# The last image's end in a four-layer hybrid network: buffers in the freed scan memory, interleaved spectral halves, and evictions split between ScalarE and VectorE

## The chip, the cores and the metric

The kernel runs on one core of one Trainium2 chip. The metric is the device time of one execution in microseconds, from launch to end; lower is better. Three runs of the kernel before took 6479.0, 6490.46 and 6488.11 us, so its median is 6488.11 us.

The engines are named as the profile names them: PE is TensorE with its matmuls, PEld its weight loads, DVE is VectorE, ACT is ScalarE, POOL is GpSimd, SP is SyncE, whose queue issues all the loads and stores here.

## What is computed

Four images of 96 channels and 64 x 64 pixels go through four layers. In short:

```python
# layer 0: group norm, input projection and 3x3 convolution, four selective scans
h = h * exp(delta * A) + (delta * u) * B;  y = sum(h * C)      # 4 directions, 192 channels, 16 states, 4096 steps
x = x + Wout @ layer_norm(y0 + y1 + y2 + y3)
# layer 1: inverted bottleneck
x = x + bn(w2 @ relu(bn(depthwise3x3(relu(bn(w1 @ x))))))
# layer 2: spectral mixing over the 4096 tokens, then a feed-forward with numbers rounded to 8 bits
X = fft(relu(bn(layer_norm(t) @ w1)))
t = t + bn(ifft(relu(X.real*rd - X.imag*id + rb) + 1j*relu(X.imag*rd + X.real*id + ib)).real @ w2)
t = t + ffn(layer_norm(t))       # relu(q(q(x) @ q(W1)) + q(b1)), then the same with W2
# layer 3: attention without softmax, so (q k^T) v = q (k^T v), then the second feed-forward
t = t + attention(layer_norm(t)); t = t + ffn(layer_norm(t))
```

## The kernel before

**Tiling.** An image is cut into 8 chunks of 512 pixels (8 rows of 64). Channels lie on partitions, pixels on the free axis; the layer-0 scan puts 32 channel pairs times 4 states on the 128 partitions.

**The long part.** `scans` walks over all scan units of all four images. POOL makes the products `db` (L1215) and half of `hc` (L1254), ACT the decays (L1225), DVE the scans (L1234) and the other half of `hc` (L1239), PE sums the states (L1275). This part stands under a hand-made order: everything else of the images (`front`, `turn`, `conv_block`, `spectral`, `layers_2_and_3`) is written as generators that yield their cost per engine, and `advance` slips their steps in beside the scan. Each of these groups of generators is a `Stage` with a width, the number of streams that run at a time.

**The end.** When the scan of the last image is over, three things are left: the rest of `conv_block` of that image, and all of its layers 2 and 3. `force` issues these steps in turn. `alone` is set by then: it gives the small products all eight PSUM banks (`turns`), and it picks other code in a few places. In this part the order on each engine is no longer by hand; the framework's scheduler places the instructions. `spare` says from where the fp32 temporaries `tmp` come: before, from the pool `beside` (tag `tmp`, ten buffers, which also hold all 8-bit and 16-bit temporaries) and from the scan's own tags `rep_d`, `rep_BC` and `hc`, of which each gives half a buffer. That is why scan names stand in rows of the last stages.

**conv_block.** A block `c` is two chunks (16 rows). `scan_outputs` makes the layer-0 result of a chunk (loads of `ypart` L679, sums L696, norm L715 to L737) and stores it to `d_x1`. `expansions` loads the 18 rows that a block needs as `xin` (L773, trace name `wd<-x`), and makes 18 groups of hidden channels by L782 into a ring of eight. `rows` does the depthwise products L805, whose results ACT evicts by L811, then the projection L821 and L822, and L825 adds the input. There is one place for `xin`, so a block is loaded only when the one before is finished. `norms` then runs `layer_norm` (L858 centres, L861 squares, L864 averages, L154 and L155 make the reciprocal root by logarithm and exponential, L872 multiplies into `xp`).

**spectral.** A 4096-point transform is done as 64 x 64: five phases, each a run of `in_turn` (PE fills a bank, an engine evicts it, two in flight). L955 multiplies by `wa1`, DVE evicts to `d` (L959). L980 with table `r1` transforms, ACT evicts to `z` (L991). L999 multiplies by the 16 tables `etab`, ACT evicts with Relu to `f` (L1003). L980 with `r2`, ACT to `v` (L1011). L1021 with the 8 tables `gtab`, ACT to `y` (L1025). The tables are loaded by L973, 256 KB each, two ahead, into five buffers. The 192 channels go in two halves, one after the other. `big` gives two buffers of 24 KB per partition in turn, so the `y` of the first half is stored to `d_half` in HBM and loaded again by layer_2.

**layer_2 and layer_3.** layer_2 is one stream per chunk: L1043 and L1044 add both halves through `wa2`, `residual` (L928) adds the input, `feed_forward` runs (norm with L870 as its last step; L884 and L905 are the products; L887 and L908 move their sums to 16 bits; L892 and L911 add the biases; L898 on DVE or L901 on ACT rounds to 8 bits; L914 adds the residual), then a layer norm, the keys and values by L1055 and L1058, and their sum over all tokens in `vk` (L1064, L1070). `product` multiplies the small matrices once. layer_3 is again one stream per chunk: L1097, `residual`, `feed_forward`, store. Both have width 3.

Of the kernel before, what the change touches and what calls it, by code (L numbers as in the profile page):

```python
# [28 lines left out]
L = H * W  # L29
# [15 lines left out]
POOL_C = (1, 3, 6, 8, 10)  # L45
TMP, IN = 10, 5
# [48 lines left out]
def hybrid_kernel(ctx: ExitStack, tc: tile.TileContext, a: dict):  # L95
# [71 lines left out]
    sp = pool("scan", bufs=2)  # L167
    bp = pool("beside", bufs=2)

# [8 lines left out]

    def big(name):
        return bp.tile([128, 6144], F32, name=name, tag="big", bufs=2)  # L180
# [6 lines left out]
    def tmp(name, shape=(128, CH), dtype=F32):  # L187

        if alone and dtype == F32:
            tag = turns(spare)  # L190
            if tag in SCAN:
                return pair(tag)[:, 0, : shape[1]]
        return bp.tile(list(shape), dtype, name=name, tag="tmp", bufs=TMP)

    def arrival(name):

        return bp.tile([128, CH], F32, name=name, tag="in", bufs=IN)
# [543 lines left out]
    def conv_block(b):  # L741
# [9 lines left out]
        def memory():  # L751
            held["w"], held["h"] = big("wd"), big("h1")
            load(held["w"][:, : 6 * NG * 32].rearrange("p (g m) -> p g m", m=32), diags)
            ring = held["h"][:, : 8 * 8 * (W + 2)].rearrange("p (s r w) -> p s r w", s=8, r=8)
            held["wd"] = held["w"][:, : 6 * NG * 32].rearrange("p (g o x m) -> p g o x m", g=NG, o=2, x=3)
            held["ring"] = ring
            at = [(held["h"], 8 * 8 * (W + 2) + n * CH) for n in range(3)]
            at += [(held["w"], 6 * NG * 32 + 18 * (W + 2) + n * CH) for n in range(2)]
            held["spare"] = [t[:, lo : lo + CH] for t, lo in at]
            yield dv(0.3)  # L760
            for edge in (0, W + 1):
                nc.vector.memset(ring[:, :, :, edge : edge + 1], 0.0)

        def expansions():

            yield from memory()
            for c in reversed(range(NCH // 2)):

                while max(2 * c - 1, 0) not in done or held.get("xin") is not None:
                    yield wait(1)  # L770
                at = 6 * NG * 32
                xin = held["w"][:, at : at + 18 * (W + 2)].rearrange("p (r w) -> p r w", r=18)
                load(xin, d_x1[im][:, 16 * c : 16 * c + 18, :])  # L773
                held["xin"] = xin
# [15 lines left out]
        def rows(c):  # L790
            h2 = []
            for q, groups in enumerate(quads):
# [3 lines left out]
                xin, here = held["xin"], [h for h, _ in ready[first : first + len(groups)]]  # L796
# [34 lines left out]
            held["xin"] = None  # L831
# [6 lines left out]
        def blocks():  # L838
            for c in reversed(range(NCH // 2)):
                while held.get("xin") is None:  # L840
                    yield wait(1)
                yield from rows(c)
# [32 lines left out]
    def feed_forward(x, weights):  # L875
# [5 lines left out]
        for m in range(3):  # L881
# [14 lines left out]
            if alone and m == 1:  # L896
                yield dv(0.75)
                nc.vector.tensor_copy(hq[:, m, :], acc, saturate=False)  # L898
            else:
                yield ac(0.65)  # L900
                nc.scalar.activation(hq[:, m, :], acc, AF.Copy, saturate=False)  # L901
# [8 lines left out]
        yield ac(0.65)  # L910
        act(acc[:C], acc[:C], AF.Identity, bias=bq[:C, 3:4])  # L911
        if alone:
            yield dv(0.9)
            nc.vector.tensor_add(x[:C], x[:C], acc[:C])  # L914
            return
        yield pe(1.4, 1)
# [22 lines left out]

    def spectral(b, hh):  # L940
# [8 lines left out]

        d = big("d").rearrange("p (h n) -> p h n", h=C)  # L950
# [7 lines left out]
        def diagonal(p, g):  # L958
            nc.vector.scalar_tensor_tensor(  # L959
# [4 lines left out]
            if g == 0:  # L964
                for at in (0, 64):
                    one = d[at : at + 1, :, 0]
                    nc.vector.tensor_add(one, one, rib[at : at + 1, hs])

        yield from in_turn(range(16), pe(0.7, 1), times, dv(0.8), diagonal)

        def table(name, g, n):
            t = arrival("tab").rearrange("p (a b) -> p a b", a=n)
            load(t, a[name][:, g * n : g * n + n, :])  # L973
            return t

        def transform(of, r):
# [8 lines left out]
        tables = ahead(2, lambda g: table("etab", g, 4), range(16))  # L985
        first = next(tables)

        z = big("z").rearrange("p (k h) -> p k h", k=64)
        yield from in_turn(
            range(C // 8), pe(0.7, 1), transform(d, "r1"), ac(1.1),  # L990
            lambda p, g: nc.scalar.copy(z[:, :, g * 8 : g * 8 + 8], p.rearrange("p (h k) -> p k h", h=8)))  # L991


        f = big("f").rearrange("p (h k) -> p h k", h=C)

        def twiddled(p, of):
            g, tab = of
            for e in range(4):
                mm(p[:, e * C : (e + 1) * C], lhsT=tab[:, e, :], rhs=z[:, g * 4 + e, :], start=True, stop=True)  # L999

        yield from in_turn(
            chain([first], tables), pe(0.7, 1), twiddled, ac(0.9),
            lambda p, of: act(f[:, :, of[0] * 4 : of[0] * 4 + 4].rearrange("p h k -> p k h"),  # L1003
                              p[:, : 4 * C].rearrange("p (k h) -> p k h", k=4), AF.Relu))
        tables = ahead(2, lambda g: table("gtab", g, 8), range(8))
        first = next(tables)

        v = big("v").rearrange("p (n h) -> p n h", n=64)
        yield from in_turn(
            range(C // 8), pe(0.7, 1), transform(f, "r2"), ac(1.1),  # L1010
            lambda p, g: nc.scalar.copy(v[:, :, g * 8 : g * 8 + 8].rearrange("p n h -> p h n"),  # L1011
                                        p.rearrange("p (h n) -> p h n", h=8)))

        yf = big("y")[:, :L]
        y = yf.rearrange("p (a b) -> p a b", a=64)
        load(yf[C:], a["zeros"][: 128 - C])

        def back(p, of):
            g, tab = of
            for e in range(8):  # L1020
                mm(p[:C, e * 64 : (e + 1) * 64], lhsT=v[:, g * 8 + e, :], rhs=tab[:, e, :], start=True, stop=True)  # L1021

        yield from in_turn(
            chain([first], tables), pe(1.2, 1), back, ac(1.1),
            lambda p, of: nc.scalar.copy(y[:C, :, of[0] * 8 : of[0] * 8 + 8].rearrange("p a b -> p b a"),  # L1025
                                         p[:C].rearrange("p (b a) -> p b a", b=8)))
        halves_of[b] = yf
        if hh == 0:
            later(d_half[im], yf[:C])
# [3 lines left out]
    def layers_2_and_3(b):  # L1033
# [3 lines left out]
        def layer_2(c):  # L1037

            x, first = load_x(d_x2[im], c), load_x(d_half[im], c)
# [4 lines left out]
            mm(p[:C], lhsT=wa2[:, 1, :], rhs=halves_of[b][:, chunk(c)], start=False, stop=bool(alone))  # L1044
# [5 lines left out]
            for half, t in enumerate(kv):  # L1050
# [6 lines left out]
                yield ac(0.6)  # L1057
                nc.scalar.copy(t[:, : 4 * C], p[:, : 4 * C])  # L1058
# [33 lines left out]
        def layer_3(c):  # L1092
# [8 lines left out]

        return [
            Stage("spectral", 1, spectral(b, 0)),
            Stage("spectral", 1, spectral(b, 1)),
            Stage("layer_2", 3, *(layer_2(c) for c in range(NCH))),
            Stage("product", 1, product()),
            Stage("layer_3", 3, *(layer_3(c) for c in range(NCH))) if b not in (1, 2) else
# [324 lines left out]
    spare += ["tmp", "rep_d", "tmp", "rep_BC", "tmp", "hc"]  # L1432
# [150 lines left out]
```

## Time and profile before

| what | us |
| --- | --- |
| the three runs | 6479.0, 6490.46, 6488.11 |
| the profiled execution | 6478.26 |
| its span, first to last instruction | 6476.4 |
| busy in the span: PE, DVE, ACT, POOL | 4756.9, 5432.5, 4244.3, 5175.7 |
| last scan sum evicted (L1286) | 6009.3 to 6009.8 |
| conv_block's rest ends | 6166.7 |
| both spectral halves end | 6305.4 |
| layer_2 and product end | 6415.8 |
| last sum of layer_3; end of the span | 6472.9; 6476.4 |

The page gives busy time per engine over the whole span, and the same in 40 slices. A row of the timeline has a start, a duration, the engine, the line, output and inputs, the count and, in brackets, how long the engine was idle before it and who ended that. Line numbers are those of the kernel before. Where a group's row has a mean, instructions that follow each other closely may start less than that apart, because their records overlap: the spacing of starts is then the better price.

### The profile page before, as it was taken

Reading aid. Unit: us, or ns where it says so; the run is one execution under the profiler, and the core shown is the slowest. Engines: PE = TensorE matmul, PEld = TensorE weight load, DVE = VectorE, ACT = ScalarE, POOL = GpSimd, SP = SyncE. Lnnn points to the kernel's source line nnn. Section 1 sums busy time; section 2 is a strip of 40 time slices with the busy share of each in tenths; the row PEclk is TensorE's granted clock in tenths of the full one; section 3 lists DMA queues with packets and bytes.
Section 4 is the critical chain, followed back from the end, with each engine's and each line's share of the span. In section 5 each row is a group of like instructions: output and inputs, shape, how many; then the busy total and the mean of one; then the engine's idle time right before and its main releaser. Section 6 shows DMA issues by size and latency. Waiting matters only on the chain. (4 is left out here: it accounts for less than half of the span.)

```text
span 6476.4 us, 84592 instructions
## 1 busy us (share of the span) xinstructions
PE 4756.9 (73%) x27804; PEld 1748.4 (27%) x27804; DVE 5432.5 (84%) x5947; ACT 4244.3 (66%) x8152; POOL 5175.7 (80%) x2743
## 2 busy tenths in 40 slices
PE   7623867757987776775688877677887776758997
PEld 2100212111224521221122254211224621112383
DVE  5979998998999889989899998978998888898123
ACT  5743777865665677887466667756665676756356
POOL 4857878789998889987899988978999888899000
PEclk9755978868998887886799988888998877979998
DMA  5644565676544544466764455466644554655131
GB/s 191 206 154 145 187 208 191 202 236 232 179 156 160 172 165 151 162 202 200 241 214 160 151 183 179 159 214 192 186 156 154 173 168 168 204 189 162 34 100 39
DMA packets 438827, 1121.43 MB, mean 173 GB/s; under 512 B 73002, under 2 KB 74768, under 8 KB 437140
## 3 DMA queue, kind: packets, MB, share of 16 engines
q1 hardware_dynamic: 438388, 1116.02, 52.1%
q8 instruction: 221, 3.62, 0.2%
q14 instruction: 218, 1.79, 0.1%
HBM read 881.28 MB, written 239.01 MB: 173 GB/s over the span
## 5 line engine op out<-in xcount | busy, mean ns | idle before, releaser
L1215 POOL TENSOR_TENSOR db<-rep_g,rep_BC 128x1024 f32<-128x1024 f32 x1536 | 3597.3, 2364 | 344.3 <-DVE ps_da L1234 232.3
L1225 ACT ACTIVATE ps_da<-rep_d,aneg 128x512 f32<-128x512 f32 x3072 | 2062.5, 691 | 437.3 <-DVE hc L1234 323.1
L1234 DVE TENSOR_TENSOR_SCAN ps_da<-ps_da,state,db 128x512 f32<-128x512 f32 x1568 | 1923.9, 1272 | 314.8 <-ACT state L1249 209.9
L1254 POOL TENSOR_TENSOR hc<-hc,rep_BC 128x1024 f32<-128x1024 f32 x640 | 1511.8, 2362 | 110.4 <-DVE hc L1234 55.7
L1275 PE MATMUL ps_y<-hc,cst 128*32 128x512 f32 x6144 | 1009.2, 735 | 626.4 <-POOL hc L1254 366.7
L1234 DVE TENSOR_TENSOR_SCAN hc<-ps_da,state,db 128x512 f32<-128x512 f32 x1120 | 1371.3, 1265 | 108.2 <-issue 41.6
L1239 DVE TENSOR_TENSOR hc<-ps_da,rep_BC 128x512 f32<-128x512 f32 x1792 | 1134.9, 674 | 0.1
L1249 ACT COPY state<-ps_da 128x1 f32<-128x1 f32 x1568 | 246.9, 157 | 502.9 <-DVE hc L1239 493.4
L1275 PEld LDWEIGHTS ps_y<-hc,cst 128*32 128x32 f32 x6144 | 144.4, 117 | 1262.2 <-POOL hc L1254 748.8
L1251 POOL COPY state<-hc 128x2 f32<-128x2 f32 x560 | 105.9, 189 | 369.7 <-DVE hc L1234 352.4
L805 PE MATMUL ps_mm<-h,wd 128*32 128x512 f32 x3192 | 367.0, 595 | 8.3 <-ACT r L154 8.3
L543 PE MATMUL ps_mm<-xp,taps 128*128 128x512 f32 x576 | 296.2, 657 | 54.4 <-ACT ua L545 22.7
L1234 DVE TENSOR_TENSOR_SCAN ps_da<-ps_da,db 128x512 f32<-128x512 f32 x224 | 261.3, 1211 | 49.6 <-ACT state L1249 29.8
L782 PE MATMUL ps_mm<-wd,w 128*32 128x512 f32 x2128 | 273.8, 628 | 38.6 <-DMA wd<-x 25.1
L1286 ACT COPY yt<-ps_y 128x512 f32<-128x512 f32 x256 | 149.1, 583 | 163.7 <-PE ps_y L1275 159.2
L594 PE MATMUL ps_mm<-xd,dtw 128*128 128x512 f32 x256 | 165.5, 737 | 102.3 <-ACT z L616 55.9
L786 ACT ACTIVATE h<-ps_mm 128x512 f32<-128x512 f32 x266 | 153.4, 597 | 60.5 <-PE ps_mm L782 58.6
L955 PE MATMUL ps_mm<-wa,xp 128*64 128x96 f32 x1728 | 136.6, 317 | 76.4 <-DVE d L959 64.6
L864 PE MATMUL ps_mm<-r,cst 128*128 128x512 f32 x208 | 145.9, 790 | 63.5 <-ACT r L861 17.5
L1234 DVE TENSOR_TENSOR_SCAN hc<-ps_da,db 128x512 f32<-128x512 f32 x160 | 186.1, 1203 | 4.9 <-ACT ps_da L1225 3.3
L609 DVE SCALAR_TENSOR_TENSOR ps_mm<-ps_mm,z 128x512 f32<-128x512 f32 x192 | 131.7, 686 | 58.3 <-ACT z L607 55.0
L543 PEld LDWEIGHTS ps_mm<-xp,taps 128*128 128x128 f32 x576 | 115.5, 208 | 230.9 <-issue 159.7
(405 smaller groups left out, 6798.8 us busy)
## 6 DMA issues: line engine op xcount, KB each, us to landing
rep_BC<-bc SPq DMA_DIRECT2D x512, 512.0 KB
rep_g<-du SPq DMA_DIRECT2D x384, 512.0 KB
rep_d<-delta SPq DMA_DIRECT2D x384, 512.0 KB
y<-yt SPq DMA_DIRECT2D x512, 128.0 KB
du<-g SPq DMA_DIRECT2D x128, 256.0 KB
delta<-z SPq DMA_DIRECT2D x128, 256.0 KB
tab<-in_etab SPq DMA_DIRECT2D x128, 256.0 KB
ypart<-y SPq DMA_DIRECT2D x72, 256.0 KB
```

The costliest lines, as they stand in the source:

```text
L543: mm(p, lhsT=taps[:, t, 0:128], rhs=window(t, c + e), start=t == 0, stop=t == 8)
L594: mm(p, lhsT=dtw[:, o + 2 * part, 0:128], rhs=xd, start=True, stop=True)
L782: mm(p[32 * n : 32 * n + 32], lhsT=w1[:, 32 * g : 32 * g + 32], rhs=xin[:, n : n + 15 : 2, 1 : W + 1], start=True, stop=True)
L786: act(h[:, :, 1 : W + 1], split(p), AF.Relu)
L805: mm(p[32 * n : 32 * n + 32], lhsT=held["wd"][:, groups[i], o, dx, :], rhs=here[i][:, :, dx : dx + W], start=dx == 0, stop=dx == 2)
L1215: nc.gpsimd.tensor_mul(x["db"], x["step"]["g"][x["i"]], both(x["step"]["BC"][x["j"]][:, 0]))
L1225: act(x["da"][e], x["step"]["d"][x["i"]][:, e], AF.Exp, scale=aneg[:, av : av + 1])
L1234: nc.vector.tensor_tensor_scan(x["h"][e][:, order], x["da"][e][:, order], x["db"][:, e, order], start, ALU.mult, ALU.add)
L1239: x["made"] = nc.vector.tensor_mul(x["hc"][:, e], x["h"][e], x["step"]["BC"][x["j"]][:, 1])
L1249: nc.scalar.copy(to[:, e : e + 1], x["h"][e][:, end : end + 1])
L1254: x["made"] = nc.gpsimd.tensor_mul(x["hc"], x["hc"], both(x["step"]["BC"][x["j"]][:, 1]))
L1275: done = mm(y[32 * q : 32 * q + 32], lhsT=const("stack"), rhs=x["hc"][:, e], start=first or (x["pass"] == 0 and x["j"] == 0), stop=last or ...
```

## The change

Only what runs behind the last scan is rewritten; the code before it has the same operations.

- The pool `scan` now lies above the pool `beside` and is closed after the last scan. In its place a pool `last` is opened, with 24 table buffers, 6 more fp32 temporaries, two buffers for `xin` and one more `big`.
- `conv_block` takes `xin` from this pool in the rest, so that two blocks may be in memory at once; `held["xin"]` becomes a dict by block.
- The three `big` buffers let both spectral halves go through the five phases together, phase by phase, first half then second half. Each table is loaded once, into its own buffer, and used by both. Both results stay in SBUF: the store to `d_half` and its loads go.
- Of the evictions to `z`, `f`, `v` and `y`, the odd ones move to DVE.
- In the feed-forward all casts to 8 bits go to DVE, as well as the last bias; the copies of keys and values go to DVE too.
- The last image's layer_2 and layer_3 have width 4.
- Temporaries of layers 2 and 3 come from the `tab` and `more` buffers.
- The scratch memory for DMAs issued by POOL is set to 1024 bytes.

In the instruction lists POOL is unchanged. In the rest of `conv_block` SP loads the first `xin`, then all 24 tables in a row, then makes the stores of `o` and of chunk 0 and loads the second `xin`.

```diff
+LAST = {"tab": 24, "more": 6}
...
-    sp = pool("scan", bufs=2)
     bp = pool("beside", bufs=2)
+    scan_room = ExitStack()
+    sp = scan_room.enter_context(tc.tile_pool(name="scan", bufs=2))
+    last_room = []
...
+    thirds = ["last", "beside", "beside"]
     def big(name):
+        if last_room and turns(thirds) == "last":
+            return last_room[0].tile([128, 6144], F32, name=name, tag="big", bufs=1)
         return bp.tile([128, 6144], F32, name=name, tag="big", bufs=2)
...
-        if alone and dtype == F32:
+        if last_room and dtype == F32:
             tag = turns(spare)
-            if tag in SCAN:
-                return pair(tag)[:, 0, : shape[1]]
+            if tag in LAST:
+                return last_room[0].tile([128, CH], F32, name=name, tag=tag, bufs=LAST[tag])[:, : shape[1]]
...
-                while max(2 * c - 1, 0) not in done or held.get("xin") is not None:
+                while max(2 * c - 1, 0) not in done or len(held["xin"]) > (1 if last_room else 0):
                     yield wait(1)
...
+                if last_room:
+                    xin = last_room[0].tile([128, 18 * (W + 2)], F32, name="xin", tag="xin", bufs=2)
+                else:
+                    xin = held["w"][:, at : at + 18 * (W + 2)]
...
-            if alone and m == 1:
+            if alone:
                 yield dv(0.75)
                 nc.vector.tensor_copy(hq[:, m, :], acc, saturate=False)
...
-        yield ac(0.65)
-        act(acc[:C], acc[:C], AF.Identity, bias=bq[:C, 3:4])
         if alone:
+            yield dv(0.4)
+            nc.vector.tensor_scalar(acc[:C], acc[:C], bq[:C, 3:4], None, ALU.add)
...
+    def copied(n, out, of):
+        if last_room and n % 2:
+            nc.vector.tensor_copy(out, of)
+        else:
+            nc.scalar.copy(out, of)
+
+    def tables(name, per, n):
+        def table(g):
+            t = arrival("tab")
+            load(t, a[name][:, g * per : g * per + per, :])
+            return t.rearrange("p (a b) -> p a b", a=per)
+        if not last_room:
+            return ahead(2, table, range(n))
+        if name not in tabs:
+            tabs[name] = [(g, table(g)) for g in range(n)]
+        return iter(tabs[name])
...
+                if last_room and of[0] % 2:
+                    nc.vector.tensor_scalar(out, p, 0.0, None, ALU.max)
+                else:
+                    act(out, p, AF.Relu)
...
-            x, first = load_x(d_x2[im], c), load_x(d_half[im], c)
+            x = load_x(d_x2[im], c)
+            first = halves_of[b, 0][:, chunk(c)] if alone else load_x(d_half[im], c)
...
-                yield ac(0.6)
-                nc.scalar.copy(t[:, : 4 * C], p[:, : 4 * C])
+                if alone:
+                    yield dv(0.6)
+                    nc.vector.tensor_copy(t[:, : 4 * C], p[:, : 4 * C])
...
+        halves = [spectral(b, 0), spectral(b, 1)]
+        if b == B - 1:
+            def both():
+                for parts in zip(*halves):
+                    for part in parts:
+                        yield from part
+                spare[:] = ["tab", "tab", "more"]
+            spectra = [Stage("spectral", 1, both())]
...
-            Stage("layer_2", 3, *(layer_2(c) for c in range(NCH))),
+            Stage("layer_2", 4 if b == B - 1 else 3, *(layer_2(c) for c in range(NCH))),
...
-    spare += ["tmp", "rep_d", "tmp", "rep_BC", "tmp", "hc"]
+    scan_room.close()
+    last_room.append(pool("last"))
+    spare += ["tmp", "more"]
...
-    nc = bacc.Bacc("TRN2", target_bir_lowering=False, num_devices=1)
+    nc = bacc.Bacc("TRN2", target_bir_lowering=False, num_devices=1, dynamic_dma_scratch_size=1024)
```

## The prediction

> **What bounds the kernel now.** I first read the page's busy tenths by slice, to see where the change can act at all.
>
> ```profile
> DVE  5979998998999889989899998978998888898123
> ACT  5743777865665677887466667756665676756356
> POOL 4857878789998889987899988978999888899000
> PEclk9755978868998887886799988888998877979998
> ```
>
> One digit is 162 us. Up to the 37th slice POOL and DVE, which run the scan, are busy for most of nearly every slice. In the last three POOL stands at 0: the scan is over, and conv_block's rest, the spectral stage and layers 2 and 3 of the last image run alone. In the instruction lists of the two programs POOL's is the same row for row, and those of PE, ACT, DVE and SP are the same in operations and order up to the last fetches of scan_outputs. So the change acts from about 6010 us on, on 466 of 6476 us. Second view: busy time by stretch, cut where the timeline shows one stage end and the next begin.
>
> ```profile
> core 0: us, PE busy (x) PEld busy (x) DVE busy (x) ACT busy (x) POOL busy (x), PEclk, DMA share, GB/s
> 6020.05:6166.69 146.64, 134.84 (x830) 50.34 (x831) 10.78 (x20) 50.24 (x78) 0.00 (x0) 0.95 0.10 31
> 6166.69:6305.39 138.70, 130.44 (x2561) 128.71 (x2561) 28.04 (x36) 78.60 (x95) 0.00 (x0) 0.99 0.34 107
> 6305.39:6345.32 39.93, 31.94 (x129) 14.60 (x128) 12.34 (x26) 25.33 (x46) 0.00 (x0) 0.87 0.18 54
> 6345.32:6383.80 38.48, 31.42 (x129) 14.48 (x127) 12.58 (x27) 24.32 (x45) 0.00 (x0) 0.87 0.15 46
> 6383.80:6413.70 29.90, 23.44 (x86) 10.59 (x84) 8.56 (x18) 16.80 (x30) 0.00 (x0) 0.83 0.12 40
> 6415.84:6437.90 22.06, 17.51 (x47) 6.92 (x47) 11.14 (x23) 17.17 (x32) 0.00 (x0) 1.00 0.02 5
> 6437.90:6473.00 35.10, 23.44 (x50) 7.53 (x50) 14.90 (x34) 26.75 (x49) 0.00 (x0) 0.79 0.16 48
> ```
>
> Rows: conv rest; both spectral halves; layer_2's waves of 3, 3 and 2 chunks; layer_3's first wave; its other two. PE limits the first two; in the layers no engine is full, so latencies and turns between engines do. The third view, the timeline, shows the stops.
>
> ```profile
> 6049.64 1.08 PE L782 MATMUL ps_y<-wd,w 128*32 128x512 f32 x8 [2.39 <-DMA wd<-x]
> 6105.21 1.94 PE L782 MATMUL ps_mm<-wd,w 128*32 128x512 f32 x8 [2.88 <-DMA wd<-x]
> 6106.92 1.93 PE L782 MATMUL ps_da<-wd,w 128*32 128x512 f32 x8
> 6122.09 1.05 PE L782 MATMUL ps_da<-wd,w 128*32 128x512 f32 x8
> 6368.63 3.78 PE L858 MATMUL ps_da<-xc,cst 96*128 96x512 f32 x4 [2.19 <-DVE xc L914]
> ```
>
> PE waits for the input block at both block starts; after the second wait the same eight matmuls start 1.71 apart instead of 0.87 (the granted clock of 6105.2 to 6110.3 is 0.52). The L858 after the feed-forward are slow too (0.55).
>
> **Part 1, conv rest: second input block, tables ahead of it on SP.** PE's own work there, counted from the list at the pitches of the timeline (eight L782 0.87, 24 L805 2.57, one full fp32 product 0.86), is 124.4 of 146.6 us; 22.2 is lost. Two losses stay: the slow start after the last y store (ten L696 in 8.0 instead of 4.3: 3.7) and the closing layer norms (6157.7 to 6166.7, 9.0 with 3.4 of work: 5.6). Of the other 12.9 I can name 0.7+2.4 at the first block and 0.6+0.7+2.9 and the slow clock's 2.5 at the second: 9.8, all of which go, since xin of a block is now loaded while the block before is at work. **Gain 10** (bounds 4 and 13). The cover: xin 1 is issued behind the ypart loads at about 6021, takes 6.2 (6043.4 to 6049.6) and is wanted only behind the five L696 and seven more products, 10 us at full rate. On SP all 24 tables, then two x2 stores, the x1 store of chunk 0 and only then xin 2. Eleven tables took 10.28 us of SP in the trace, 0.93 each: done near 6045, store near 6051 (it waits for L737's result anyway), xin 2 in SBUF near 6060. PE has 61.8 us of products before it wants xin 2, which is 6086 with the slow start: 26 us of room. Should it be gone, every us of delay costs one.
>
> **Part 2, spectral.** Tables resident: 24 of 48 loads go; in the trace they held PE up by 1.1 us (L999), so alone that is worth 1. Halves in turn: PE work per half is 16 groups of times at 0.985, 12+12 of transform at 0.93, 16 of twiddled at 0.915, 8 of back at 1.36: 63.6, twice 127.2. The stage lasts 138.7; what is lost is at phase borders, where the first product waits for the last eviction (0.7 to 2.3 each), and in v, where ACT's 1.04 per group exceeds PE's 0.93. With the other half between, the last eviction lies behind 11 to 15 us of PE work. I allow 1.3 for the start: 128.5. **Gain 10** (5 to 11).
> Half the evictions, 48, move to DVE. [...] The rows say 1.04 for ACT's v copy, [...]0.67 for a DVE product out of PSUM (L1239) and 0.85 for a strided 384-wide one (L959). I take 0.7 to 1.0 for the new copies. Two engines taking turns have 1.83 us per pair of groups, so both prices hide; cost 0. DVE would have to exceed 1.83 to show.
>
> **Part 3, layer_2: waves of 4+4, not 3+3+2.** The measured waves (29.9 for two chunks, 38.5 to 39.9 for three) put 9 to 10 us on a chunk, so four unchanged would take 48. Off ACT per chunk: two hq casts (L901, three of them started at 0.53 spacing), one L911 (0.65), two kv copies (0.48). On DVE per wave of four: 12 biases and 12 casts, about 0.33 each: 7.9 against ACT's 12 x 0.5 + 8 x 0.53 = 10.2, with ACT now waiting for DVE to free the acc buffers. Step by step: the first ln of a wave at +9.0 (second wave, three chunks) moves to +11.6 by one more pair and one L858; four ln/exp at 1.17 end at 16.3; first acc to last cast 8.9: 25.2; first residual sum 26.5; four L858, four L864, ln/exp, xp: 36.8 at full clock; kv and vk 5: 41.8.
> [...] The rows show clock 0.50 to 0.55 for about 5 us after each feed-forward, with PE busy 4.77 of 10 us before it. Now 24 instead of 18 short products fill that stretch, hardly enough; by the row the wave is 44.5. I take 44, nearer the row. Two waves 88 against 108.3: **gain 20** (10 to 25). The `half` store and its eight reloads delayed nothing (the first L1043 has no wait): 0.
>
> **Part 4, layer_3.** The same sums: wave 1 has its last cast at 21.6; the sums and three residuals, all on DVE, end at 28.2, wave 2's last cast at 45.4, last sum at 49.1, the store 3.4 as now: 52.5 against 60.6 (6415.8 to 6476.4). All eight xc loads go out together, so the 4.7 us DVE wait for xc at 6442.66 goes too. **Gain 8** (2 to 13).
>
> **Nothing:** the smaller scratch. The page lists only SP's queue and two instruction queues, so no DMA goes through the POOL queue. The first tiles in the freed scan memory wait for its last users; all are done by 6019.3, when SP gets past the y store that it waits for already.
>
> **Sum:** 10+10+20+8 = 48. The profiled run took 6478.26, its span 6476.4: 6430. The median shown, 6488.11, is 9.9 above it, and all four executions average 6484; I forecast 6484-48 = **6436**.
>
> **Rivals.**
> - A, as summed: 6436, its own range 6424 to 6450; chance 0.50.
> - B, the layers gain little: feed-forward is a ping-pong of ACT and DVE, and four chunks in step leave PE idle and slow longer. For: clock 0.55 and the waits of L914 for L911 (16.2 us in all). Against: the linear fit. Waves near 49, layers gain 10: 6454. Chance 0.20.
> - C, PE stays at full clock and conv loses nothing: waves 41.8, layer_3 11, conv 13: 6425. Chance 0.23.
> - D, slower than before: all scan buffers change place in SBUF, since the pool that outlives them now lies below. If an address matters to POOL or DVE, the scan pays for 6000 us: POOL's products at 2364 ns would need 0.8% more (19 ns) to eat all 48 us; with 1.2% it is 6508. For it: the scan is the bound. Against: same shapes, order and engines, and no row in which equal instructions differ by buffer. Chance 0.03.
> - E, the tables starve xin 2: free until 2.3 us per table, and it loses only beyond 4.3; the row says 0.93. At 2.8 each 12 us goes: 6448. Chance 0.04.
>
> Range 6418 to 6458: A and most of B and C, plus the 11 us by which the three runs differ. A difference below 0.2%, 13 us, is no change that can be told. Of D nearly all falls slower; small gains of B with D's milder form give the middle: faster 0.92, same 0.04, slower 0.04.
>
> **What would show it.** No PE wait for DMA in the second block and conv rest near 136 us; spectral near 128.5, PE idle only at its ends; two layer_2 waves of 42 to 46, layer_3 near 52; the first 6010 us unchanged within 10. Wrong if the span before the last scan moves by over 0.3%, if xin 2 lands after PE wants it, or if a wave of four exceeds 48.

## The result and the profile after

Four runs of the changed kernel took 6432.73, 6448.08, 6440.66 and 6439.49 us, median 6440.07; the kernel before, run beside it, has a median of 6486.1. The ratio is 0.993 with an interval of 0.9913 to 0.9948: faster by 46 us, where 48 had been summed. The profiled execution took 6432.73, its span 6430.9.

First the busy tenths of the changed kernel by slice, one digit for 161 us.

```profile
DVE  5979998998999889999899998978999789898345
ACT  5743777865665677887466667856666577665435
POOL 4757878789999889987899988978999789899200
PEclk9755978878998877896799988888998787878999
```

POOL again stops before the last two slices. There DVE has risen and ACT fallen by a tenth or two, which is the moved work. The scan's slices look as before. Now busy time of the changed kernel by stretch: conv_block's rest, spectral, layer_2's two waves (the second with `product`), layer_3.

```profile
core 0: us, PE busy (x) PEld busy (x) DVE busy (x) ACT busy (x) POOL busy (x), PEclk, DMA share, GB/s
6022.03:6162.87 140.84, 136.26 (x830) 48.60 (x831) 10.77 (x20) 50.26 (x78) 0.00 (x0) 0.97 0.20 69
6162.87:6291.60 128.73, 128.73 (x2562) 128.02 (x2562) 69.71 (x84) 41.32 (x48) 0.00 (x0) 0.99 0.06 17
6291.60:6335.02 43.42, 37.85 (x168) 18.81 (x167) 24.50 (x56) 22.29 (x40) 0.00 (x0) 0.96 0.12 37
6335.02:6379.55 44.53, 37.79 (x175) 18.94 (x173) 25.23 (x60) 22.29 (x40) 0.00 (x0) 1.00 0.18 54
6379.55:6430.90 51.35, 36.31 (x96) 14.27 (x96) 32.84 (x80) 30.37 (x56) 0.00 (x0) 0.93 0.10 31
```

In spectral PE is now busy for the whole stretch, with some 0.7 us of layer_2's first product in it. In the layers ACT's share has fallen below DVE's, and the granted clock is 0.93 to 1.00 where it was 0.79 to 1.00. By stage in us, cut at the first product of each:

| stage | before | after | gain | forecast |
| --- | --- | --- | --- | --- |
| start to first L705 of the rest | 6020.1 | 6022.0 | -2.0 | 0 |
| conv_block's rest | 146.6 | 140.8 | 5.8 | 10 |
| spectral | 138.7 | 128.1 | 10.6 | 10 |
| layer_2 and product | 110.4 | 88.6 | 21.8 | 20 |
| layer_3 | 60.6 | 51.4 | 9.2 | 8 |
| sum | | | 45.5 | 48 |

Three stages came out close to their sums, conv_block's rest did not. There the changed kernel's timeline has no PE wait for DMA left behind its start:

```profile
6022.03 9.34 PE L705 MATMUL ps_mm<-ypart,cst 128*128 128x512 f32 x10 [3.83 <-DMA ypart<-yt]
...
6036.36 1.02 PE L835 MATMUL ps_mm<-wd,w 128*96 128x512 f32 x2
6037.31 1.08 PE L795 MATMUL ps_da<-xin,w 128*32 128x512 f32 x8
6038.32 1.13 PE L724 MATMUL ps_mm<-yrow,cst 128*128 128x512 f32 x2
6039.28 1.02 PE L725 MATMUL ps_mm<-yrow,cst 128*128 128x512 f32 x2
6040.14 2.74 PE L834 MATMUL ps_mm<-h,w 128*96 128x512 f32 x6
...
6091.34 1.38 PE L795 MATMUL ps_da<-xin,w 128*32 128x512 f32 x8
```

L795, L705, L724, L725, L834 and L835 here are L782, L696, L715, L716, L821 and L822 of the kernel before. The last row is the second block's first group: nothing in brackets, where before stood 2.88 for DMA. But see the spacings of the five rows in the middle: 0.95, 1.01, 0.96, 0.86. Among their own kind such products start 0.87 (L795) or 0.86 apart. One group of 32-column products (eight L795) between full ones thus costs 0.3 us more than it does in a row of such groups.

### The profile page after: what moved, and what is told of

It is laid out like the page before. It is cut to its first block, busy times and chain, and to the rows that moved or that the text cites. A ratio compares the mean times of both kernels' runs of the same rounds, so it can differ in the third digit from the quotient of the medians.

```text
span 6430.9 us, 84514 instructions
## 1 busy us (share of the span) xinstructions
PE 4759.6 (74%) x27804; PEld 1744.9 (27%) x27804; DVE 5504.2 (86%) x6059; ACT 4172.2 (65%) x8040; POOL 5176.0 (80%) x2743
## 5 line engine op out<-in xcount | busy, mean ns | idle before, releaser
L1274 POOL TENSOR_TENSOR db<-rep_g,rep_BC 128x1024 f32<-128x1024 f32 x1536 | 3597.5, 2364 | 344.3 <-DVE ps_da L1293 230.2
L818 PE MATMUL ps_mm<-h,wd 128*32 128x512 f32 x3192 | 367.1, 595 | 8.3 <-ACT r L155 8.3
L795 PE MATMUL ps_mm<-wd,w 128*32 128x512 f32 x2016 | 256.2, 624 | 32.2 <-DMA wd<-x 20.2
L990 PE MATMUL ps_mm<-wa,xp 128*64 128x96 f32 x1728 | 136.8, 319 | 72.5 <-DVE d L995 61.1
```

The lines of the kernel that those rows point to most:

```text
L795: mm(p[32 * n : 32 * n + 32], lhsT=w1[:, 32 * g : 32 * g + 32], rhs=xin[:, n : n + 15 : 2, 1 : W + 1], start=True, stop=True)
L818: mm(p[32 * n : 32 * n + 32], lhsT=held["wd"][:, groups[i], o, dx, :], rhs=here[i][:, :, dx : dx + W], start=dx == 0, stop=dx == 2)
L1274: nc.gpsimd.tensor_mul(x["db"], x["step"]["g"][x["i"]], both(x["step"]["BC"][x["j"]][:, 0]))
```

## The experiments

All are the changed kernel with one edit, except `xin_bufs1` with two and `best` with three; `after_again` is the changed kernel once more. A total moves by 10 us and more with the scan (the first L705 of the rest began between 6016.9 and 6042.1 us over twelve profiles), so stages are compared, in us, each from one profile.

| run | ten L705 | conv rest | spectral | layer_2, product | layer_3 |
| --- | --- | --- | --- | --- | --- |
| before | 8.2 | 146.6 | 138.7 | 110.4 | 60.6 |
| changed | 9.3 | 140.8 | 128.1 | 88.6 | 51.4 |
| one_xin | 9.2 | 140.1 | 128.5 | 88.6 | 51.5 |
| xin_bufs1 | 9.2 | 144.1 | 128.1 | 88.6 | 51.5 |
| tabs4 | 8.1 | 139.7 | 127.6 | 90.3 | 53.2 |
| seq_halves | 4.9 | 136.4 | 137.7 | 88.6 | 53.2 |
| evict_act | 4.9 | 136.5 | 127.6 | 90.3 | 51.5 |
| width3 | 4.9 | 136.4 | 128.5 | 99.8 | 54.7 |
| casts_act | 9.2 | 140.7 | 128.1 | 100.5 | 54.0 |
| heads | 4.9 | 136.5 | 128.4 | 83.9 | 53.2 |
| filler | 5.0 | 136.4 | 128.7 | 88.6 | 51.5 |
| after_again | 4.9 | 136.5 | 128.4 | 88.6 | 51.5 |
| best | 4.9 | 135.7 | 128.6 | 82.5 | 51.3 |

Apart from xin_bufs1, conv rest of the changed kernel has two values, some 4 us apart, that go with the time of the ten L705 and with nothing that was edited. The layers too show steps of 1.7 us (88.6 or 90.3, 51.4 or 53.2) in stages that an edit did not touch. The last section shows where both steps come from.

### Is it the second place for xin?

```diff
-                while max(2 * c - 1, 0) not in done or len(held["xin"]) > (1 if last_room else 0):
+                while max(2 * c - 1, 0) not in done or len(held["xin"]) > 0:
```

> The changed kernel with one place for xin again; the tables still go ahead on SP. In the changed kernel conv_block's rest takes 140.8 us. Theory: the second place took PE's waits at the two block starts away, which the prediction put at 9.8 us; the trace of the changed kernel also shows 0.15 us at each change of PE between 32-column products and full ones, of which this version makes 16 in place of 27, so 1.7 us comes back. Conv rest 147 (145 to 149), with PE waits for xin at both block starts. Rival, that the second place is worth little and the gain is from elsewhere (own buffer, order of loads): conv rest within 2 us of 140.8. The stages behind it stay within 1 us of the changed kernel (128.7, 88.6, 51.4).

Measured: 140.1, no wait for xin. The theory, as it was put, fell: the order in which the program asks for `xin` is worth nothing here. The pool still had two buffers, and SP, meeting a free one, sent the load out at 6054.3, 46 us before the next stores of `o` (6100.7); in the changed kernel it left at 6056.3. So the second run also takes the second buffer away:

```diff
-  xin = last_room[0].tile([128, 18 * (W + 2)], F32, name="xin", tag="xin", bufs=2)
+  xin = last_room[0].tile([128, 18 * (W + 2)], F32, name="xin", tag="xin", bufs=1)
```

> The changed kernel with one place for xin in the program order and also one buffer for it (in one_xin the pool still gave two). In the five profiles with the change so far, conv_block's rest takes 140.1 to 140.8 us where the ten first L705 run slow (9.2 to 9.3 us) and 136.4 to 136.5 where they run fast (4.9). Theory: what took the waits away is that the load of xin no longer has to wait for the last reader of the block before (VectorE's addition, L838), as SP meets no full buffer; with one buffer the load again stands behind that reader, PE waits 2 to 3 us for DMA at each block start, and conv rest is 147 (145 to 150) with a slow start or 142.5 (141 to 145) with a fast one. Rival, that the waits went because xin no longer shares a buffer with the weights: no such waits, conv rest 139.5 to 141 (slow start) or 135 to 137 (fast).

Measured: 144.1, 3 below the expectation, with one wait instead of two. SP's queue in this run (start, time of the issues, queue):

```profile
6017.55 0.42 SPq L787 DMA_DIRECT2D xin<-x  x1
...
6094.41 0.80 SPq L444 DMA_DIRECT2D x<-o  x2
6095.64 0.33 SPq L787 DMA_DIRECT2D xin<-x  x1
```

And PE in it:

```profile
6100.19 1.49 PE L795 MATMUL ps_mm<-xin,w 128*32 128x512 f32 x8 [2.82 <-DMA xin<-x]
```

The second load stands behind the stores of `o` again and PE waits for it. The first goes out at once, since `xin` no longer lies inside the tile `wd`, where the last block's input still was; SP's queue before shows it behind the last addition L825 (6042.0 to 6042.9):

```profile
6042.55 0.80 SPq L435 DMA_DIRECT2D x<-o  x2
6043.39 0.44 SPq L773 DMA_DIRECT2D wd<-x  x1
```

What conv rest loses over 124.9 us of products at full spacing, counted from the rows (the prediction had 124.4):

| | start (L705) | PE waits | other spacing | sum |
| --- | --- | --- | --- | --- |
| before | 3.7 | 13.7 | 4.4 | 21.8 |
| xin_bufs1 | 4.7 | 10.2 | 4.3 | 19.2 |
| one_xin | 4.7 | 5.4 | 5.1 | 15.2 |
| changed | 4.9 | 5.4 | 5.7 | 16.0 |

A buffer of its own takes 3.5 us of waits away, the second buffer 4.8. "Other spacing" in the changed kernel is mostly changes between 32-column and full products: 4.7 us at 32 changes, 0.15 each. Before, seven such changes cost 1.3, and 2.5 were the three groups at half clock behind the second wait. one_xin makes 18 changes, which cost 2.8, but it was only 0.6 better in this column. What it saved there it lost in one stretch: from 6110.0 to 6145.7 its twelve groups of L795 and nine of L818, 33.6 us at full spacing, took 35.7. There the rows of two groups alternate, as they do in neither of the other two:

```profile
6110.00 0.64 PE L795 MATMUL ps_y<-xin,w 128*32 128x512 f32 x3
6110.02 0.62 PE L818 MATMUL ps_mm<-h,wd 128*32 128x512 f32 x1
6110.46 0.61 PE L795 MATMUL ps_y<-xin,w 128*32 128x512 f32 x3
```

Why such groups take longer stays open.

### Do the tables hold up the second xin?

```diff
-            load(t, a[name][:, g * per : g * per + per, :])
+            to = t.rearrange("p (a b) -> p a b", a=per)
+            for lo in range(0, per, per // 4 if last_room else per):
+                hi = lo + (per // 4 if last_room else per)
+                load(to[:, lo:hi, :], a[name][:, g * per + lo : g * per + hi, :])
```

> The changed kernel with each of the 24 tables loaded in four loads of 64 KB. Nothing else changes. In the changed kernel the tables leave SP at 0.73 us each and the second xin goes out at 6056.3, 35 us before PE starts on it. Theory 1, a load costs SP its 0.73 us whatever its size: 96 loads take 70 us, the x1 store of chunk 0 and the second xin come some 45 us later, and conv_block's rest grows by 8 to 20 us with a PE wait for xin. Theory 2, 0.73 us is 256 KB at the 390 GB/s that the trace shows there, so bytes set it: the second xin moves by less than 10 us and conv_block's rest stays at 140 to 141 (slow start) or 136 to 137 (fast).

Measured: the 96 loads occupied SP for 50.3 us, 0.52 each, so a load of a quarter of the size costs SP 0.52 instead of 0.71 and the cost is mostly per load, as theory 1 has it; but conv rest did not grow (139.7), as theory 2 has it. In this run SP's queue reads:

```profile
6035.88 20.26 SPq L970 DMA_DIRECT2D tab<-in_etab  x37
6059.66 0.80 SPq L444 DMA_DIRECT2D x<-o  x2
6060.51 1.87 SPq L970 DMA_DIRECT2D tab<-in_etab  x4
6063.66 0.34 SPq L444 DMA_DIRECT2D x<-xc  x1
6064.04 1.97 SPq L970 DMA_DIRECT2D tab<-in_etab  x4
6068.66 0.33 SPq L787 DMA_DIRECT2D xin<-x  x1
6069.03 9.35 SPq L970 DMA_DIRECT2D tab<-in_etab  x19
```

The stores and `xin` are placed among the tables: outside the hand-made order the scheduler seems to lay out SP's queue by the time at which things are ready. So the second `xin` left 33.9 us after the first L705, as in the changed kernel (34.2). So whether late tables could hold up `xin` was not tested by this edit: it made them later and left `xin` in time.

### What makes spectral shorter?

```diff
-                for parts in zip(*halves):
+                for parts in halves:
...
-    thirds = ["last", "beside", "beside"]
+    thirds = ["beside", "beside", "beside", "beside", "last"] + 5 * ["beside"]
```

> The changed kernel with the two spectral halves one after the other; the tables stay resident and the evictions stay split between ACT and DVE. Theory: what the interleaving takes away are the phase borders. Before, the stage took 138.7 us; of that 1.1 (tables) and 2.6 (24 v evictions on ACT, 0.11 over PE's group) do not come back, so 135 (133 to 137.5) in place of 128.7. Rival, that resident tables and split evictions carry the gain: 131 or less.

Measured: 137.7, 0.2 above the expected interval. Interleaving is worth 9.6 of the 10.6; resident tables and split evictions together 1.0, so even less than the expectation left for them. PE waits at all eight phase borders of this run, 0.8 to 1.2 us each and 7.8 in all, and at none inside the stage of the changed kernel. Two of the eight:

```profile
6208.59 1.15 PE L1009 MATMUL ps_mm<-cst,f 128*64 128x64 f32 x32 [0.98 <-DVE f L1039]
6221.16 1.54 PE L1063 MATMUL ps_mm<-tab,v 128*96 128x64 f32 x16 [1.15 <-ACT v L959]
```

```diff
-        if last_room and n % 2:
+        if False:
             nc.vector.tensor_copy(out, of)
...
-                if last_room and of[0] % 2:
+                if False:
                     nc.vector.tensor_scalar(out, p, 0.0, None, ALU.max)
```

> The changed kernel with all evictions of z, f, v and y on ACT; halves interleaved. Theory: the v copies on ACT (1.04 us) exceed PE's group (0.93) in 24 groups, 2.6 us, and nothing else shows: spectral 131.3 (130 to 132.5) in place of 128.7. Rival, [...]the move to DVE brought nothing[...], so spectral is 128.7 or less here. Second rival, one engine cannot keep up at all: above 135.

Measured: 127.6. The theory fell and the rival holds: the move to DVE brings nothing. tabs4, with the evictions split and the same full clock throughout the stage, has 127.6 too; the changed kernel's 128.1 holds 3.4 us at half clock near the stage's start. Groups by line of this run on ACT (busy time, mean ns, idle before):

```profile
L1041 ACT ACTIVATE f<-ps_da 128x384 f32<-128x384 f32 x16 | 13.3, 833 | 0.9
L959 ACT COPY v<-ps_da 128x512 f32<-128x512 f32 x12 | 12.0, 1056 | 0.0
L959 ACT COPY y<-ps_da 96x512 f32<-96x512 f32 x8 | 8.3, 1035 | 2.5 <-PE ps_da L1063 2.5
```

ACT does not pause in `v`: its 24 copies take 25 us against 22.3 of PE. But the 2.8 us of lag did not stop PE, which is busy for all of the 127.6, and ACT waits for PE again in `y`. In the changed kernel the same copies on both engines:

```profile
L959 ACT COPY v<-ps_da 128x512 f32<-128x512 f32 x6 | 6.4, 1073 | 4.9 <-PE ps_da L1009 4.9
L959 ACT COPY z<-ps_da 128x512 f32<-128x512 f32 x6 | 3.5, 586 | 7.7 <-PE ps_da L1009 7.7
...
L957 DVE COPY v<-ps_da 128x512 f32<-128x512 f32 x6 | 6.2, 1036 | 5.4 <-PE ps_da L1009 5.4
L957 DVE COPY z<-ps_da 128x512 f32<-128x512 f32 x6 | 4.1, 691 | 6.9 <-PE ps_da L1009 6.9
```

For `z` ACT is the faster, 0.59 us a copy against 0.69 on DVE. For `v` both take 1.04 to 1.07. A copy to `z` writes eight elements that lie together, one to `v` writes every element 96 apart; `y`, with elements 64 apart, takes 1.03 and 1.04. That the stride of the writes sets the time on either engine fits these rows, but no run changed it alone.

### Width, or work off ACT?

```diff
-            Stage("layer_2", 4 if b == B - 1 else 3, *(layer_2(c) for c in range(NCH))),
+            Stage("layer_2", 3, *(layer_2(c) for c in range(NCH))),
...
-            Stage("layer_3", 4 if b == B - 1 else 3, *(layer_3(c) for c in range(NCH))) if b not in (1, 2) else
+            Stage("layer_3", 3, *(layer_3(c) for c in range(NCH))) if b not in (1, 2) else
```

> The changed kernel with width 3 in layer_2 and layer_3; casts, last bias and key/value copies stay on DVE. Theory: the width brought most of the layers' gain; waves of 3, 3 and 2 chunks have 28.4, 28.4 and 18.9 us of PE work and some 8 of stops each, so layer_2 up to the end of product is 98 to 106 (88.6 in the changed kernel, 110.4 before) and layer_3 56 to 59 (51.4 and 60.6). Rival, that the work taken off ACT brought it: layer_2 at 92 or less, layer_3 at 53 or less.

Measured: 99.8, as the theory has it, and 54.7, 1.3 below its interval.

```diff
-            if alone:
+            if alone and m == 1:
                 nc.vector.tensor_copy(hq[:, m, :], acc, saturate=False)
...
-            nc.vector.tensor_scalar(acc[:C], acc[:C], bq[:C, 3:4], None, ALU.add)
+            act(acc[:C], acc[:C], AF.Identity, bias=bq[:C, 3:4])
...
-                if alone:
+                if False:
                     nc.vector.tensor_copy(t[:, : 4 * C], p[:, : 4 * C])
```

> The changed kernel with the casts to 8 bits of the first and third part, the last bias and the copies of keys and values on ACT as before; width 4 stays. width3 measured layer_2 at 99.8 us and layer_3 at 54.7 with all of this on DVE, before has 110.4 and 60.6, the changed kernel 88.6 and 51.4. Theory (the prediction's own figure): four chunks in step with ACT's work unchanged take 48 us a wave, so layer_2 with product is 96 to 99 and layer_3 55 to 58. Rival, that at width 4 other chunks cover ACT's latency: layer_2 at 91 or less, layer_3 within 1 us of 51.4.

Measured: 100.5, 1.5 above the expected interval, and 54.0, 1.0 below it. Width and moved work count alike: with one of them layer_2 goes from 110.4 to about 100 (casts_act keeps the width, width3 the moved work), with both to 88.6. Neither rival holds. Both runs also keep the new temporaries and the halves that stay in SBUF; no run has these without width and moved work, so their own share is not shown. Busy time of layer_2 with product, then layer_3, of casts_act:

```profile
6294.54:6395.03 100.49, 82.47 (x342) 40.02 (x341) 35.49 (x76) 63.81 (x120) 0.00 (x0) 0.90 0.13 40
6395.03:6449.00 53.97, 37.72 (x96) 14.68 (x96) 26.14 (x56) 42.60 (x80) 0.00 (x0) 0.86 0.10 30
```

The same two stretches of the kernel before:

```profile
6305.39:6415.84 110.45, 87.62 (x342) 40.16 (x341) 34.49 (x75) 66.45 (x121) 0.00 (x0) 0.86 0.15 47
6415.84:6476.40 60.56, 40.95 (x96) 14.45 (x96) 26.03 (x56) 43.92 (x80) 0.00 (x0) 0.85 0.12 36
```

Read PE's busy time at an equal count of products. Before it is 87.6 + 41.0 = 128.6 us, with casts_act 120.2, in the changed kernel (its rows above, 6290.93 to the end) 112.6. So of the 31.0 us gained in the layers 15.0 are shorter stops and 16.0 are the same products in less time. Nearly all of the latter is clock: PE worked at half clock for 34.9 us before and for 6.8 in the changed kernel. If a product there takes twice its time, as the eight L782 behind the second wait did (1.71 for 0.87), half of the difference is gained, an estimated 14.0. Here, filling PE's stops paid twice.

### Fill the first feed-forward

```diff
+        if beside is not None:
+            yield from beside
         yield pe(1.4, 1)
...
-            yield from feed_forward(x, ffn[0])
+            yield from feed_forward(x, ffn[0], head(c + 4) if alone and c < 4 else None)
```

`head` is L1088, L1089 and the residual of a chunk.

> The changed kernel with the first products of layer_2's second wave (L1088, L1089 and the residual after them, four chunks, 13.8 us of PE) made inside the feed-forward of the first wave, between its two products. Theory: PE idles 5.6 us in the feed-forward of the first wave and runs the centring products behind it at half clock (2.2 us lost), both because it has too little to do there; filled, both losses go: layer_2 with product is 80 to 83.5 in place of 88.6, with no slow row in the first wave. Rival, that DVE is the pace of the feed-forward and four more residual sums on it delay the rounding: 86 or more.

Measured: 83.9, 0.4 above the expected interval, with no slow row in the first wave. The 13.8 us in the expectation were mis-sized: four chunks of two products at 0.86 are 6.9. In the changed kernel the products behind the first feed-forward read

```profile
6317.33 1.55 PE L871 MATMUL ps_mm<-xc,cst 96*128 96x512 f32 x2 [1.08 <-DVE xc L927]
6318.68 3.16 PE L871 MATMUL ps_da<-xc,cst 96*128 96x512 f32 x4
```

and with heads

```profile
6326.95 1.12 PE L871 MATMUL ps_mm<-xc,cst 96*128 96x512 f32 x2
6327.94 1.12 PE L871 MATMUL ps_da<-xc,cst 96*128 96x512 f32 x2
```

The wait and the half clock are gone; the granted clock is 1.00 from 6298.0 to 6340.0. The first wave takes 44.8 instead of 44.1 with 6.9 us more work in it; the second, with product, 39.1 instead of 44.5.

### The start of conv_block's rest, and a faster version

```diff
                 p = bank()
+                for n in range(4 if (b, c, name) == (B - 1, 0, "ident") else 0):
+                    mm(p, lhsT=const("ident"), rhs=cst[:, :CH], start=n == 0, stop=n == 3)
                 for n, s in enumerate(of):
```

> The changed kernel with four fp32 products without a reader (3.4 us) put on PE before the first L705 of the rest, where it waits 3.6 us for DMA. In ten profiles so far the ten L705 took 8.1 to 9.3 us in six and 4.9 us in four, behind the same idle time of 3.6 to 4.0 us. Theory, the idle time lets the clock drop[...]: with the gap filled the L705 always take 4.9 and conv_block's rest 136.4. Rival, the clock drops for another reason (the loads of the tables at the same time, the kind of product): 8 us or more is still seen here or in best.

> The changed kernel with three edits: layer_2's second heads inside the first feed-forward (as in heads), the program order of one_xin (two buffers, but one place in the order), and four fp32 products without a reader put before the first L705 of the rest, where PE waits 3.6 us for DMA. Stage times expected from the runs so far: conv_block's rest 135 to 136.5 if the products keep the clock up (ten L705 in 4.9 us), 139 to 141 if they do not (9.2 us); spectral 128; layer_2 with product 83 to 84.5; layer_3 51.4 or 53.1. The sum of the stages is 399 to 402, against 408.9 in the profile of the changed kernel. The whole time should lie 5 to 12 us below that of after_again, but the start of the first L705 has ranged from 6016.9 to 6040.6 us over the profiles, so that interval may hold zero.

> The changed kernel once more, beside best on the same chip. Expected 6430 to 6450 us, ratio to before 0.991 to 0.995. Stages: conv rest 140 to 141 with a slow start or 136.5 with a fast one, spectral 128 to 128.7, layer_2 88.6 or 90.3, layer_3 51.4 or 53.1.

Measured: both kernels with filled gaps ran the ten L705 at full clock (5.0 and 4.9 us). But so did after_again with its gap, and five of the eleven profiles without a filler did, so these two cases prove little by themselves. That the filled gap is what kept the clock up is an inference from the other eleven (last section): there it stayed up where PE was busy for 1.50 us or more of the emptier step of the gap, and fell at 1.40 or less. The filler costs nothing that shows: conv rest takes 136.4 with it and 136.4 to 136.5 in the five with the fast start.

The whole time of best has a median of 6430.0 us (six runs), 0.9915 of before (0.990 to 0.9931); after_again 6440.1 (five runs), 0.9934 (0.9923 to 0.9946). The intervals overlap, so by whole times best is not shown to beat the changed kernel. By stages, both at full clock from the start, it is 398.1 against 405.0 us: 0.8 less in conv rest, 6.1 less in layer_2 (82.5, half a us better than expected). Busy time of best in its layer_2 with product, then of after_again:

```profile
6300.21:6382.70 82.49, 73.58 (x343) 37.15 (x342) 50.22 (x116) 44.68 (x80) 0.00 (x0) 1.00 0.13 39
```

```profile
6307.03:6395.66 88.63, 76.31 (x343) 37.92 (x342) 50.23 (x116) 44.59 (x80) 0.00 (x0) 0.98 0.15 45
```

PE is idle for 8.9 us instead of 12.3, and its clock is 1.00.

## Why the prediction came out

**The time** was right, 6436 forecast and 6440 measured, and of its cases A: 45.5 of 48 us came, stage by stage near their terms except one. That the total is so near is in part luck: conv rest fell 4.2 short, the other three gave 3.6 more than their terms, and the start of the first L705, which differs by up to 25 us between profiles, happened to differ by 2.0.

**Conv rest, 5.8 for 10: a term was mis-sized.** The prediction named 9.8 us of waits and low clock and said "all of which go". Between before and the changed kernel PE's waits fell by 8.3, and the 2.5 us of the three groups at half clock behind the second wait are gone: 10.8, so these did go. What the sum lacked is what came back. Changes of product rose by 3.4, from 1.3 to 4.7, and other small steps by 0.4; and the start, taken as equal, cost 1.2 more in this execution. At an equal start the gain is 7.0; after_again, with the fast start, has 136.5 for conv rest, near the 136 of the prediction, but by that start. The prediction priced L795 at 0.87 wherever it stands; laid between full products it costs about 1.2. That waits go because `xin` is loaded while the block before works was right, and the numbers for it too: the second load left at 6056.3 and PE wanted it at 6091.3 (6086 forecast). What allows it is the buffers, 3.5 and 4.8 us of waits, not the new condition in the code.

**Spectral, 10.6 for 10: right, and for the reason given.** seq_halves puts 9.6 on the interleaving, 7.8 of it waits at the phase borders. The remaining 1.0 is near the 1.1 that the prediction gave the tables, though no run took the tables alone. Moving 48 evictions was costed at 0 and is 0 (127.6 us in evict_act and in tabs4). The prediction took 0.7 to 1.0 for the copies on DVE; they are 0.69 (`z`), 0.82 (`f`) and 1.04 (`v`). Its remark that `v` on ACT loses time against PE was wrong once halves alternate.

**layer_2, 21.8 for 20: right.** The waves took 44.1 and 43.0 (44.5 with product), for 44. Its price for four unchanged chunks, 48, was about right too: casts_act took 49.5 a wave. On the clock the row that the prediction leant on came true in one wave of two. Both waves have the same gaps in their feed-forward, none above 1.1 us, and yet L871 ran at half clock behind the first and at full clock behind the second. The loss in the first wave was 1.8 us (starts 1.35 and 3.00 apart for 0.86 and 1.72), and heads took it away. In seq_halves, with the same 1.08 us wait in front of L871, it is the other way round (starts 1.12 and 1.80 apart in the first wave, 1.53 and 2.82 in the second), so it is in part luck that both together, 87.1, came out at the 88 of the prediction. What the prediction does not say is that nearly half of the gain in the layers, an estimated 14.0 of 31.0 us, is clock, not stops.

**layer_3, 9.2 for 8: right**, with 51.4 for 52.5. casts_act is 6.6 us below before and width3 5.9, more than 9.2 together. In part both count the same gain: DVE's 4.7 us wait for `xc`, which the prediction said would go, is in neither.

**The rivals.** B fell: waves are 44, not 49. C was nearer in the second wave, but conv rest gave 6, not 13. D: the scan shows no loss. POOL's product `db` takes 2364 ns in both kernels, where D needed 19 more. The first L705 began at 6028.4 on average in the twelve profiles with the change; the median of before in the last comparison, 6484.1, less the 458.2 us that its profiled run spent from there to the end, gives 6025.9, within the scatter. E did not come: the tables left SP at 0.71 us each. It was also built on a fixed order of SP's queue; tabs4 showed that the order gives way.

## What to carry to other kernels

When stages alternate on an engine that limits them, price the alternation too: see in the rows what a product costs between products of another shape (here 0.15 us a change, 4.7 in all). Here the load was early where a buffer of its own was free at the time its queue reached it (3.5 and 4.8 us of waits); where the program asks for it was worth nothing (140.1 in one_xin, 140.8). Stops of PE were worth more than their length here: with 15.0 us of shorter stops came 16.0 of the same products in less time. So the first thing to look for is independent work to put into them.

## What the hardware showed beyond that

Equal waits did not give equal clocks. Ten L705 behind the same gap, in xin_bufs1 and then in after_again:

```profile
6016.90 9.16 PE L705 MATMUL ps_mm<-ypart,cst 128*128 128x512 f32 x10 [3.62 <-DMA ypart<-yt]
```

```profile
6042.13 4.92 PE L705 MATMUL ps_mm<-ypart,cst 128*128 128x512 f32 x10 [3.63 <-DMA ypart<-yt]
```

Six of eleven profiles show the first (8.1 to 9.3 us), five the second, some 4 us apart; the changed kernel itself shows either. The clock's records show where the two part. In all thirteen the granted clock is 1.00 or 0.50 and nothing between, every piece but the cut ones at a trace's ends is a whole multiple of 3.41 us long, and one grid fits the 400 or so changes of an execution to 0.01 us. The gap lies across two steps of that grid. They are, for xin_bufs1 and then for after_again, as stretches with busy times (behind the length of 3.41 us stands PE's busy time; the third number from the end is the granted clock):

```profile
6011.97:6015.38 3.41, 1.31 (x14) 0.12 (x3) 0.00 (x0) 0.78 (x1) 0.00 (x0) 1.00 0.14 41
6015.38:6018.79 3.41, 1.89 (x3) 0.89 (x4) 0.00 (x0) 0.00 (x0) 0.00 (x0) 0.50 0.45 154
```

```profile
6036.97:6040.38 3.41, 1.52 (x14) 0.24 (x6) 0.00 (x0) 0.78 (x1) 0.00 (x0) 1.00 0.16 49
6040.38:6043.79 3.41, 1.66 (x4) 0.67 (x4) 0.00 (x0) 0.00 (x0) 0.00 (x0) 1.00 0.47 143
```

In the six slow profiles PE is busy for 0.74 to 1.40 us of the emptier step, and the next step is at half clock; in the five fast ones it is busy for 1.50 to 1.55, and the clock stays. So in these eleven the clock behind the same gap went with where the grid lay. The 1.40 and 1.50 us are no limit for other products: in layer_2 of the changed kernel a step with 1.92 us of PE work, before the slow L871, is followed by half clock, and one with 1.80 (at 6348.6) is not. What decides in general is not shown.

The other step in the table is one more piece of 3.41 us at half clock in which PE is busy throughout: layer_2 has one such piece where it takes 88.6 us and two where it takes 90.3, and layer_3 one for 51.4 and two for 53.2. Each cost 1.7 us there, half its length: PE's busy time in layer_2 is 76.3 us in the changed kernel and 78.0 in evict_act, in layer_3 36.3 and, in seq_halves, 38.0. In spectral such a piece cost less: in the changed kernel the first 64 products L990 take 4.8 us with it, in evict_act 4.0 without. A single profile of these stages can thus hold steps of 1.7 or 4 us that no edit made.
